# First set of the last product: its sums of h by chunks through PSUM, its weight sums behind the mask group's, the mask count later

## The chip, the core and the metric

The kernel runs on one core of a Trainium2 chip. The metric is device time in microseconds (us), the median of several runs. One further execution was recorded by the hardware profiler; its own time and its span, from the first to the last instruction, are given beside the median below. All instants in this document are microseconds from the start of that span.

The engines are called by their names: TensorE (PE in the profile; PEld is its weight load), VectorE (DVE), ScalarE (ACT), GpSimd (POOL) and SyncE (SP), which here only issues DMA transfers.

## The reference

Everything is fp32. There are 2 x 1024 tokens of 512 features, and the inner size of the gated layer is 1792.

```python
xn = layernorm(x)
block_mask = mask.reshape(16, 32, 16, 32).sum(axis=(1, 3)) > 0
s  = xn @ (weight * spread(block_mask)).T         # 512 -> 512
nx = xn * rsqrt(mean(xn ** 2) + 1e-5) * ln_w
h  = silu(nx @ gate_w.T) * (nx @ up_w.T)          # 512 -> 1792
g  = silu(h @ down_w.T)                           # 1792 -> 512
out = x + s * g
```

## The kernel before

**Products.** Every large product is split twice into 2 x 2 blocks, and at each of the two levels seven products of sums of blocks stand in for eight products of blocks (a Strassen scheme in Winograd's form). The outer level gives seven sets, numbered 1 to 7; inside a set, the inner level again gives seven products, also numbered 1 to 7. Numbers 1, 2 and 3 take blocks as they are on the side of the data; 5, 6, 7 and 4 take sums, and there 6 is formed from 5 and 4 from 6. On the weights' side 1, 2 and 4 take blocks and 5, 6, 3, 7 take sums.

**Stages.** Groups 0 to 6 are seven slices of gate and up weights, group 7 is the masked linear layer. First all groups run sets 1 and 2, then each group runs sets 6, 5, 7, 3, 4. One set of one group is an *instance*: seven products of 128x128 by 128x512 over seven positions. The last instances are those of group 7, the *mask group*. Then comes the *last product*, h by the down weights: seven sets in the order 1, 2, 6, 5, 7, 3, 4, of 25 products each (the very last ones are cut into narrower parts). For each set its h is loaded back from memory (`load_h`), its weights too (`load_d`), `inner_h` makes the four sums of h, and `inner_d` the four sums of the weights, on GpSimd.

**Order.** Each piece of work is put down with a position, `at(pos, fn, ...)`; at the end all pieces are sorted by position and issued in this order, so the order on every engine is written by hand. One position is about one product of TensorE. `END` is the position of the first product of set 1 of the last product; `D(o)(k)` is the position of product k of the o-th set. An engine works through its own pieces strictly in that order and waits where an input isn't there or a target is still read.

**Buffers.** One large tile `mem` of SBUF is cut into slots of 128x512, which are reused: `F["vc"]`, `F["a1"]` and so on are first slots of rings. PSUM banks are taken in turn from X (3 banks), Y (2), Z (1) and V (2). X, Y and Z hold running products; V holds whatever is short-lived: gates, copies of weights, the mask count `pm`. VectorE and ScalarE read and write PSUM here, GpSimd works on SBUF alone.

**Inside an instance.** Product 1 starts bank X, 5 starts Y, ScalarE copies X to Z (`seed`), 2 adds to Z, 6 to X. Then VectorE (ScalarE in sets 1 and 5) takes a *snapshot* of X and of Y, after which 7 and 4 add to X and 3 to Y, and VectorE reads each *total*. So the product 7 must wait for the snapshot of X, and product 3 for the snapshot of Y. In the mask group, set 5 ends in tiles v5, and GpSimd adds v5 and the running tiles acc into a third place (`summed`); set 7 then overwrites acc, which its VectorE totals may do only after that GpSimd sum has read it, and GpSimd adds again. These are the eight *mask sums* of GpSimd, all 128x512.

**What the change touches.** `mask_blocks` (L302): one small product that counts the mask by blocks of 32, and VectorE's compare. `inner_h` (L528): the sums of h, one instruction of 128x1536 each (three slots). `inner_d` (L514): the weight sums, four GpSimd instructions of 128x384. The placing of these for the o-th set stands in the loop over `DOWN`. Earlier users of the slots matter too: `h_sum` is GpSimd's sum of h in groups 0 to 6, stored to memory from L458, and the tiles vc of group 6 lie in `F["vc"]`.

Of the kernel before, what the change touches and what calls it, by code (L numbers as in the profile page):

```python
# [11 lines left out]
ALU = mybir.AluOpType  # L12
# [19 lines left out]
def tile_masked_linear_gated_ffn(  # L32
# [11 lines left out]
    nc = tc.nc  # L44
# [23 lines left out]
    def at(pos, fn, *args):  # L68
        events.append((pos, len(events), fn, args))
# [11 lines left out]
    F = first_slot  # L81
# [6 lines left out]
    def slots(i, n):  # L88
        return mem[:, i : i + n, :]
# [3 lines left out]
    def bank(tag, name):  # L93
        return ps.tile([P, W], F32, tag=tag, name=name, bufs=PSB[tag])

    def add(eng, o, a, b, op=ALU.add):
        eng.tensor_tensor(o, a, b, op)  # L97

    dve, pool, act = nc.vector, nc.gpsimd, nc.scalar
# [379 lines left out]
    K3 = G // 2  # L479
    assert G == 2 * K3 + 1  # L480
    dq, ds, dh, dt = {}, {}, {}, {}
# [32 lines left out]
    def inner_d(q, i):  # L514
        s = slots(i, 3).rearrange("p s w -> p (s w)").rearrange("p (m k w) -> p m k w", m=4, k=K3)
        a11, a21, a12, a22 = (dq[q][:, k : k + K3, r : r + P] for k in (0, K3) for r in (0, P))
        ds[q] = {5: s[:, 0], 6: s[:, 1], 3: s[:, 2], 7: s[:, 3], 1: a11, 2: a12, 4: a22}
        return [lambda: add(pool, s[:, 0], a21, a22), lambda: add(pool, s[:, 1], s[:, 0], a11, ALU.subtract),
                lambda: add(pool, s[:, 2], a12, s[:, 1], ALU.subtract), lambda: add(pool, s[:, 3], a11, a21, ALU.subtract)]
# [8 lines left out]
    def inner_h(q, m, i):  # L528
# [3 lines left out]
                7: lambda: (b22, b12), 4: lambda: (b21, dt[q, 6])}[m]()  # L532
        add(dve, t, a, b, ALU.subtract)

    fin, at_later = {}, []

    def load_final(R, Hh, i, slot_s, slot_x):
# [117 lines left out]
    END = 7 * N  # L655
# [109 lines left out]
    for i, (R, K) in enumerate(QUADS):  # L765
        at(62, load_mask, R, K)
        at(68 + 1.5 * i, mask_rows, R, K)
    at(76, mask_blocks)
    at(120, rms_store)
    for t in range(NTT):  # L770
        at(END + 13, rms_rows, t)
# [9 lines left out]
    def D(o):  # L781
        return lambda k: free[25 * o + k] if 25 * o + k < 25 * len(DOWN) else free[25 * o + k - 1] + 1

    H0, H1 = F["B1"], F["B6"]
    TS = [F["B7"] + K3 * k for k in range(5)]
    first_t = F["q"] - 1, F["a1"]
    b11, b12, b21, b22, e0, e1 = (0, 0, K3), (1, 0, K3), (0, K3, 2 * K3), (1, K3, 2 * K3), (0, G - 1, G), (1, G - 1, G)
    QD, later = (F["a1"] + 4, F["acc"], F["s"] + 5), {}
    for o, q in enumerate(DOWN):
        if o == 0:  # L790
            parts = [(p, 7 * where[4, 6] + 4 * k) for k, p in enumerate((b11, b12, b22, b21, e0, e1))]
        elif o == 1:
            parts = [(p, END - 22 + 7 * p[0]) for p in (b11, b21, e0, b12, b22, e1)]
        else:
            d = D(o - 2)
            parts = [(b11, d(4)), (b12, d(4) + 0.1), (b21, d(14)), (b22, d(21)), (e0, d(25) + 1), (e1, d(25) + 1.1)]
        for part, pos in parts:
            at(pos, load_h, q, (H0, H1)[o % 2], part)
        for k, m in enumerate((5, 6, 7, 4)):
            pos = END + (-26, -17, -8, -5)[k] if o == 0 else D(o - 1)((3, 8, 12, 18)[k])  # L800
            at(pos + 0.3, inner_h, q, m, first_t[k] if o == 0 and k < 2 else TS[(4 * o + k + 3) % 5])
        at((END - 29.8, END - 14, END + 7)[o] if o < 3 else D(o - 2)(4), load_d, q, QD[o % 3])

        def weight_sums(q=q, i=F["q"] + 2 - 3 * (o % 2), o=o):
            for k, fn in enumerate(inner_d(q, i)):
                later[o, k] = fn
        for k in range(4):
            pos = END + (-22, -18, -11, -9)[k] if o == 0 else D(o - 1)(10) + 2.5 * k
            if k == 0:
                at(pos, weight_sums)  # L810
            at(pos, lambda o=o, k=k: later[o, k]())
# [81 lines left out]
```

## Time and profile before

| what | value |
|---|---|
| median of 3 runs (lowest, highest) | 521.33 us (521.26, 521.42) |
| the profiled execution, its own time | 520.12 us |
| its span | 518.3 us |
| TensorE busy | 507.8 us, 98% of the span |
| VectorE busy | 384.5 us, 74% |
| GpSimd busy | 341.8 us, 66% |
| ScalarE busy | 177.8 us, 34% |
| memory moved | 121.59 MB, mean 235 GB/s |
| granted TensorE clock | full |

In a line of a timeline the first number is the start, the second the length; then come the engine, the line of the kernel, the operation, and written<-read by the program's names. "xN" says that N like instructions are merged. In brackets stand the idle time of the engine ahead of the instruction and what ended it. Almost all additions have the line L97, since one helper issues them; they are told apart by engine, tiles and sizes. A line of the chain of waits has start, length and what was at work; "issue" is time in which nothing that the profile shows was waited for. The stretch around the last instances of the mask group lies between 330 and 368 us, the mask count at 85 us, the last product from 362 us on.

### The profile page before, as it was taken

How to read it: one execution, taken by the hardware profiler on the slowest of the kernel's cores; microseconds unless marked ns; L12 is line 12 of the kernel's file. 1: busy time of each engine (PE TensorE's matmuls, PEld its weight loads, DVE VectorE, ACT ScalarE, POOL GpSimd, SP SyncE). 2: the span in 40 equal slices, each digit the busy share in tenths (PEclk: the TensorE clock that was granted, in tenths of full speed). 3: DMA queues.
4: the chain of work that ended last, by engine and by line, in shares of the span. 5: the costliest groups of instructions: out<-in, count | busy, mean ns of one | idle time of the engine just before them, and what ended most of it. 6: DMA issues, size and time to landing. Idle time of an engine off the chain costs nothing. (4 is left out here: it accounts for less than half of the span.)

```text
span 518.3 us, 4933 instructions
## 1 busy us (share of the span) xinstructions
PE 507.8 (98%) x1277; PEld 231.2 (45%) x1277; DVE 384.5 (74%) x583; ACT 177.8 (34%) x340; POOL 341.8 (66%) x280
## 2 busy tenths in 40 slices
PE   8899999999999999999999999998999999999997
PEld 8444544444444444444444444433444444444444
DVE  5897789876886969789696978979646654467826
ACT  3657644542536344353634433320101101001111
POOL 4422239852695978869597789989553564739960
PEclk9999999999999999999999999999999999999999
DMA  8435465459158485666988466498997599476472
GB/s 293 153 122 203 163 219 212 178 204 330 75 204 288 158 283 182 231 237 212 390 313 298 168 239 245 184 333 316 330 381 272 183 355 347 158 254 195 157 236 82
DMA packets 60460, 121.59 MB, mean 235 GB/s; under 512 B 5760, under 2 KB 13328, under 8 KB 58384
## 3 DMA queue, kind: packets, MB, share of 16 engines
q1 hardware_dynamic: 60144, 120.75, 65.9%
q10 hardware_dynamic: 288, 0.52, 0.3%
q8 instruction: 10, 0.16, 0.1%
q14 instruction: 18, 0.15, 0.1%
HBM read 75.11 MB, written 46.15 MB: 234 GB/s over the span
## 5 line engine op out<-in xcount | busy, mean ns | idle before, releaser
L97 POOL TENSOR_TENSOR mem<-mem 128x512 f32<-128x512 f32 (+4 forms) x243 | 306.4, 1285 | 139.1 <-ACT mem L264 45.6
L343 PE MATMUL x<-mem 128*128 128x512 f32 x448 | 214.5, 595 | 1.8 <-DVE mem L97 1.7
L343 PEld LDWEIGHTS x<-mem 128*128 128x128 f32 x448 | 83.3, 190 | 109.7 <-issue 85.2
L97 DVE TENSOR_TENSOR mem<-x,mem 128x512 f32<-128x512 f32 x136 | 91.7, 683 | 40.9 <-PE x L343 39.3
L343 PE MATMUL y<-mem 128*128 128x512 f32 x224 | 114.6, 593 | 1.6 <-DVE mem L97 1.5
L97 DVE TENSOR_TENSOR mem<-mem 128x512 f32<-128x512 f32 (+2 forms) x64 | 83.8, 1315 | 7.7 <-PE dx L570 4.2
L570 PE MATMUL dx<-mem 128*128 128x512 f32 x174 | 78.3, 592 | 0.0
L97 DVE TENSOR_TENSOR mem<-y,mem 128x512 f32<-128x512 f32 x96 | 65.7, 684 | 10.7 <-PE y L343 8.8
L343 PEld LDWEIGHTS y<-mem 128*128 128x128 f32 x224 | 42.0, 190 | 53.9 <-issue 46.5
L350 ACT COPY z<-x 128x512 f32<-128x512 f32 x55 | 31.5, 573 | 99.8 <-PE x L343 92.4
L343 PE MATMUL z<-mem 128*128 128x512 f32 x112 | 57.3, 593 | 0.5 <-ACT z L350 0.5
L570 PEld LDWEIGHTS dx<-mem 128*128 128x128 f32 x174 | 33.1, 190 | 41.6 <-issue 40.7
L570 PE MATMUL dy<-mem 128*128 128x512 f32 x98 | 44.5, 592 | 0.0
L404 ACT ACTIVATE gate<-mem 128x512 f32<-128x512 f32 x56 | 33.1, 601 | 28.1 <-DVE mem L97 23.7
L409 DVE TENSOR_TENSOR mem<-gate,mem 128x512 f32<-128x512 f32 x56 | 38.1, 681 | 4.5 <-POOL mem L97 3.7
L543 POOL TENSOR_TENSOR mem<-mem 128x512 f32<-128x512 f32 x16 | 24.9, 1565 | 17.3 <-DMA mem<-s_dram 17.0
L343 PEld LDWEIGHTS z<-mem 128*128 128x128 f32 x112 | 21.0, 190 | 26.7 <-issue 23.7
L553 ACT ACTIVATE silu<-mem 128x512 f32<-128x512 f32 x15 | 9.0, 602 | 64.6 <-DVE mem L97 48.3
L97 DVE TENSOR_TENSOR mem<-z,mem 128x512 f32<-128x512 f32 x41 | 28.0, 682 | 4.3 <-PE z L343 3.0
L570 PEld LDWEIGHTS dy<-mem 128*128 128x128 f32 x98 | 18.6, 190 | 23.4 <-issue 23.2
L97 DVE TENSOR_TENSOR mem<-dx,mem 128x512 f32<-128x512 f32 x16 | 11.0, 690 | 20.1 <-PE dx L570 20.1
L570 PE MATMUL dz<-mem 128*128 128x512 f32 x56 | 25.2, 592 | 0.0
(69 smaller groups left out, 280.2 us busy)
## 6 DMA issues: line engine op xcount, KB each, us to landing
h_dram<-mem SPq DMA_DIRECT2D x98, 256.0 KB, 2.1
mem<-h_dram SPq DMA_DIRECT2D x28, 768.0 KB, 6.4
mem<-in_gu SPq DMA_DIRECT2D x42, 256.0 KB, 4.1
acc_dram<-mem SPq DMA_DIRECT2D x8, 1024.0 KB, 4.0
mem<-acc_dram SPq DMA_DIRECT2D x8, 1024.0 KB, 4.9
s_dram<-mem SPq DMA_DIRECT2D x16, 256.0 KB, 2.4
mem<-s_dram SPq DMA_DIRECT2D x16, 256.0 KB, 6.6
mem<-in_x_t SPq DMA_DIRECT2D x16, 256.0 KB, 6.5
```

The costliest lines, as they stand in the source:

```text
L97: eng.tensor_tensor(o, a, b, op)
L343: nc.tensor.matmul(st[key], weights(g, q, m), operand(q, m), start=first and not (key == "z" and seeded), stop=True, skip_group_check=True)
L350: nc.scalar.copy(st["z"], st["x"])
L404: nc.scalar.activation(gate[key], t(), AF.Silu)
L409: nc.vector.tensor_mul(a(), gate[key], b())
L543: at_later.append(lambda: nc.gpsimd.tensor_tensor(s_tile, s_tile, rms_bc[t], ALU.mult))
L553: nc.scalar.activation(b[0][:, part], y[:, part] if source is None else source(), AF.Silu)
L570: nc.tensor.matmul(st[key], w(), b(), start=first and key != "z", stop=True, skip_group_check=True)
```

## The change

Three things change, all in order and slots; what is computed stays.

- **Sums of h of set 1.** The sums numbered 5 (b12 - b11) and 7 (b22 - b12) share the operand b12. Before, each was one 128x1536 instruction, at END - 25.7 and END - 7.7. Now they are made by three chunks of 128x512 each: ScalarE copies the chunk of b12 into a V bank, and VectorE makes both sums of that chunk from the bank, at END - 22.95, - 15.95 and - 8.95. Sum 6 goes from END - 16.7 to END - 1.95, sum 4 from END - 4.7 to END + 7.5. Sum 7 lies in the slots of the old vc, where it was in those of B7.
- **Weight sums of set 1.** The four GpSimd instructions go from END - 22, - 18, - 11, - 9 to END - 6, - 4.8, + 2, + 4, which is behind all eight mask sums. The load that feeds them keeps its place.
- **The mask count** goes from position 76 to 79.5, four products later.

On the engines this adds three ScalarE copies, and six VectorE sums of 128x512 for two of 128x1536. No transfer is added, removed or reordered.

```diff
+    def first_h(q, k, i5, i7):
+        st = {}
+        def in_bank():
+            st[0] = bank("V", f"h_{k}")
+            nc.scalar.copy(st[0], dh[q][:, 1, k, :])
+        def sums():
+            for m, i in ((5, i5), (7, i7)):
+                dt.setdefault((q, m), slots(i, K3))
+            add(dve, dt[q, 5][:, k, :], st[0], dh[q][:, 0, k, :], ALU.subtract)
+            add(dve, dt[q, 7][:, k, :], dh[q][:, 1, K3 + k, :], st[0], ALU.subtract)
+        return in_bank, sums
...
-    at(76, mask_blocks)
+    at(79.5, mask_blocks)
...
-    first_t = F["q"] - 1, F["a1"]
+    first_t = {5: F["q"] - 1, 7: F["vc"], 6: F["a1"], 4: TS[1]}
...
         for k, m in enumerate((5, 6, 7, 4)):
-            pos = END + (-26, -17, -8, -5)[k] if o == 0 else D(o - 1)((3, 8, 12, 18)[k])
-            at(pos + 0.3, inner_h, q, m, first_t[k] if o == 0 and k < 2 else TS[(4 * o + k + 3) % 5])
+            if o:
+                at(D(o - 1)((3, 8, 12, 18)[k]) + 0.3, inner_h, q, m, TS[(4 * o + k + 3) % 5])
+            elif m in (6, 4):
+                at(END + {6: -1.95, 4: 7.5}[m], inner_h, q, m, first_t[m])
+        if o == 0:
+            for k in range(K3):
+                in_bank, sums = first_h(q, k, first_t[5], first_t[7])
+                at(END - 24.4 + 7 * k, in_bank)
+                at(END - 22.95 + 7 * k, sums)
...
         for k in range(4):
-            pos = END + (-22, -18, -11, -9)[k] if o == 0 else D(o - 1)(10) + 2.5 * k
+            pos = END + (-6, -4.8, 2, 4)[k] if o == 0 else D(o - 1)(10) + 2.5 * k
```

## The prediction

> **What bounds the kernel now.** I read the page first, then TensorE's timeline for its gaps, then the chain of waits around each gap, then the timelines of the engines named there.
>
> From the page, the busy shares:
>
> ```profile
> PE 507.8 (98%) x1277; PEld 231.2 (45%) x1277; DVE 384.5 (74%) x583; ACT 177.8 (34%) x340; POOL 341.8 (66%) x280
> ```
>
> TensorE is the bound. Each product is two rows, which start 0.43 us apart when nothing holds them (0.86 us a product), so time can only come from the places where that beat breaks. TensorE's timeline (start, length, idle before it and what ended it), in three stretches:
>
> ```profile
> 83.21 1.13 PE L343 MATMUL x<-mem 128*128 128x512 f32 x2
> 85.10 0.41 PE L304 MATMUL pm<-mask_sums,blockones 128*128 128x64 f32 x2 [0.76 <-DVE mem L409]
> 85.34 0.65 PE L343 MATMUL y<-mem 128*128 128x512 f32 x1
> ...
> 347.35 1.02 PE L343 MATMUL x<-mem 128*128 128x512 f32 x2
> 349.39 0.70 PE L343 MATMUL x<-mem 128*128 128x512 f32 x1 [1.02 <-DVE mem L97]
> ...
> 358.93 1.02 PE L343 MATMUL x<-mem 128*128 128x512 f32 x2
> 361.42 0.70 PE L343 MATMUL y<-mem 128*128 128x512 f32 x1 [1.47 <-DVE mem L97]
> ```
>
> Counted by beat: the product at 347.35 should be followed at 348.21, the next comes at 349.39 (1.18 lost); at 358.93 it should be 359.79, it is 361.42 (1.63); the mask count pm should start at 84.18 (its forerunner's second row starts at 83.75), it starts at 85.10 (0.92). After a gap the first row takes 0.53 instead of 0.43 (0.10 more). From 362.4 to 511 no gap is shown.
>
> The chain of waits says where the two late gaps come from:
>
> ```profile
> 337.68 5.86 DMA mem<-in_down
> ...
> 344.62 1.28 POOL mem L97
> 345.90 0.02 issue
> 345.92 0.07 DVE mem L97
> 345.99 0.54 issue
> 346.53 2.81 DVE mem L97 x2
> 349.34 0.04 issue
> 349.39 1.13 PE x L343 x2
> ...
> 354.66 6.72 DVE mem L97 x5
> 361.38 0.04 issue
> 361.42 1.12 PE y L343 x2
> ```
>
> First gap: GpSimd stands at a weight sum of the last product until its load lands at 343.54; the mask group's sum behind it ends at 345.90 and frees the tile that VectorE then overwrites; VectorE's next instruction is a 128x1536 sum of h (2.20); only behind it comes the snapshot that the product at 349.39 needs. Second gap: two 128x1536 sums of h (2.41, 2.57) stand in front of the y snapshot.
>
> [...] (GpSimd, equal sums):
>
> ```profile
> 338.42 2.80 POOL L97 TENSOR_TENSOR mem<-mem 128x512 f32<-128x512 f32 x1
> 350.77 1.27 POOL L97 TENSOR_TENSOR mem<-mem 128x512 f32<-128x512 f32 x1
> ```
>
> The 2.80 lies over the first h sum (337.85 to 340.08). [...] here the sums with a PSUM input take 0.68 beside a busy GpSimd. [...] the trace has 0.68 and, undisturbed, 1.75 (364.98). [...]
>
> **The change part by part.**
>
> (1) Mask count four products later. One pm product, one VectorE compare, no DMA. pm now waits for a PSUM bank of the V pair, last read by the gate product at 84.27 to 84.95. In the new order y, x, x, y precede pm: it comes at 84.18 + 4 x 0.86 = 87.6, when bank and sums are ready. Gain 0.92. Its own 0.24 stays. VectorE's wait of 0.59 in front of the compare goes too, and what follows it stands about a microsecond earlier, as TensorE now asks. The compare ends at about 88.9; GpSimd's masking, its first reader, begins at 94.16.
>
> (2) Sums of h for sets 5 and 7 by chunks. Removed: two 128x1536 VectorE sums in the mask group (2.23 and 2.41). Added: three ScalarE copies of 0.58 (price of the like copies at L257) and six VectorE sums of 0.68, 0.60 apart, so 3.6 on VectorE in three bursts of 1.2. The copies are free: ScalarE works 6.3 of the 32.6 us from 329.8 to 362.4. Behind the first copy (about 338.6) stands the x copy of 339.82, which still waits for TensorE then. The first burst waits for more: its second sum writes the slots of the old vc, still read by group 6's last h sum on GpSimd and by a store. That store was issued at 337.27 and took 2.2 to land (339.4); the GpSimd sum would end at 338.42 + 1.27 = 339.7 now that no 1536 sum blocks it. So the burst ends near 340.6, and the next VectorE instruction was not due before 340.68. The later bursts fall at about 346.5 and 352.5, each behind the snapshot that TensorE needs next.
>
> (3) The other h sums. Set 6 moves to near the end: it follows the snapshot x of the last instance and runs about 358.5 to 360.3 (2.5 at most if blocked); its reader is the ninth product from the first of set 1. Set 4 moves into the last product, near 365.3 to 367.1 beside TensorE; its reader comes near 379. Behind it on VectorE stand two sums for the second set, needed beyond 380, and on SP the rms rows, whose slots it reads (issue at 370.30 before; TensorE's own reading ends near 369 now), so no queue moves back.
>
> (4) Weight sums behind the mask sums. Four GpSimd sums of 0.99 each leave the middle of eight 128x512 sums. The mask sums then follow their inputs: the first at 341.0 (its copy on ScalarE ends at 340.89), the one that freed VectorE at 345.90 by 342.3; the last waits for VectorE at about 354.3 and ends at 355.6 instead of 361.89. The weight sums then run 355.6 to about 359.6, or 361 if set 6's sum blocks one. The first is needed at 362.8, the second at 366.2. The load itself stays where it was on SP.
>
> TensorE's new beat: the product of 349.39 comes at 348.21 (its snapshot ends near 346.5), that of 361.42 at 358.50 (its snapshot ends at 356.8), the last product begins at 359.36 instead of 362.38. Gain: 1.18 + 0.10 + 1.63 + 0.10 = 3.01, plus 0.92, is 3.93. The small gaps of each group (0.3 with its slow row at 330.07) are left.
>
> Unknown costs. A sum with one input in PSUM and one in SBUF is in the trace (0.68), so is the copy; both ends are the same. That pm's gain of 0.92 passes through 240 us of other groups isn't shown: I take all of it, since the chain of every later gap goes back to TensorE's own products; the ends are 0 and 0.92. VectorE's burst beside TensorE: 0 to 0.5 lost; I take 0.
>
> Profiled execution: span 518.3, so 514.4, with the 1.8 around it (520.12) 516.2. The runs' median is 521.33, 1.21 above that execution; so 521.33 - 3.93 = 517.4.
>
> **The rivals.**
>
> A, a new small wait: a burst meets a snapshot that TensorE needs. Against it, the margins of 1.7 at both former gaps; for it, the small gaps in all groups, where VectorE is a few tenths late. Costs 0.3 to 1.2: 517.7 to 518.6.
>
> B, pm's gain is swallowed: a late engine between 85 and 330 makes TensorE wait later. Against it, results of that time are done well ahead: GpSimd's first masked weights at 95.22, for products that begin near 104. 518.3.
>
> C, slower: the store of the old vc lands late. On SP it stands right in front of the big load:
>
> ```profile
> 337.27 0.32 SPq L458 DMA_DIRECT2D h_dram<-mem  x1
> 337.68 0.38 SPq L489 DMA_DIRECT2D mem<-in_down  x1
> 338.50 0.32 SPq L458 DMA_DIRECT2D h_dram<-mem  x1
> ```
>
> The store of 338.50 took 6.1 to land, behind that load. If the first shared this fate (near 345), VectorE would stand 5 us with four instructions behind the burst's last sum, the x_2003, y_2048 and x_2038 totals among them; the product of 345.63 would wait for the last until about 347.8, 2.2 late, and the gain fall to 1.7 (519.6). Every further microsecond counts in full: from a landing at about 347.1 the change loses, and at 349 the time is 523. Against it: SP issues in order, and the store has 0.4 us of lead.
>
> D, the change does nothing: both gaps stay because VectorE is late from its total work. Against it, VectorE is idle for 5.0 of the 32.6 us there, and of the 9.4 us of its four 1536 sums 2.4 are over the undisturbed 1.75 each. 521.3.
>
> **How the numbers follow.** This forecast 0.63 (517.4, own range 517.0 to 517.7); A 0.12; B 0.08; a partial loss in C to 520 0.03; D 0.05; slower by C or an unseen wait 0.09. A range of 516.8 to 519.4 leaves the last three and a little out. A measurement of this kernel can tell about 0.2% (1 us) from no change. Faster than 520.3: 0.63 + 0.12 + 0.08 + 0.03 = 0.86, less 0.01 of A that comes out worse than its price: 0.85; same, D and that, 0.06; slower 0.09.
>
> **What would show it.** Right: no TensorE gap over 0.2 between 331 and 362; pm with no idle before it; the first dx product near 358.4 (both gains); GpSimd's eighth mask sum ending near 354.7, no 2.8 sums there. Wrong: a VectorE idle of microseconds in front of the second chunk sum (C), dy waiting for GpSimd's first weight sum, or gaps that return to TensorE before 330 (B).

## The result, and the profile after

The changed kernel takes 516.44 us (median of 4 runs, 516.12 to 516.81), the kernel before 521.3 (4 runs: the three known ones and one of 519.86). The ratio is 0.9913, 95% interval 0.9895 to 0.9932: 4.5 us faster, between 3.5 and 5.5. (The medians are 4.9 apart, the means of the same runs 4.5; the run of 519.86 moves the mean and hardly the median.) The forecast was faster, 517.4 within 516.8 to 519.4; the time lies 0.36 us below that range. The profiled execution took 516.81 with a span of 515.0; against the profiled execution of before, 518.3, that is 3.3.

The page after, TensorE's busy time and the others':

```profile
PE 507.4 (99%) x1277; PEld 231.5 (45%) x1277; DVE 383.6 (74%) x587; ACT 179.3 (35%) x343; POOL 339.3 (66%) x280
```

TensorE's timeline after, at the three places where it had gaps:

```profile
87.53 0.33 PE L304 MATMUL pm<-mask_sums,blockones 128*128 128x64 f32 x2
...
347.11 1.88 PE L343 MATMUL x<-mem 128*128 128x512 f32 x4
...
358.26 1.02 PE L343 MATMUL y<-mem 128*128 128x512 f32 x2
359.12 1.02 PE L586 MATMUL dx<-mem 128*128 128x512 f32 x2
```

No line has an idle time in brackets. The mask count comes at 87.53, without a wait in front of it. The four rows from 347.11 are two products; between them, where 1.18 us were lost, nothing is lost now. The two rows from 358.26 are the product in front of which 1.63 were lost. The last product begins at 359.12, 3.26 earlier than before.

VectorE after, at the first former gap:

```profile
344.80 0.69 DVE L97 TENSOR_TENSOR mem<-z,mem 128x512 f32<-128x512 f32 x1 [0.24 <-PE z L343]
345.59 0.69 DVE L97 TENSOR_TENSOR mem<-x,mem 128x512 f32<-128x512 f32 x1
346.20 0.68 DVE L97 TENSOR_TENSOR mem<-h,mem 128x512 f32<-128x512 f32 x1
```

The total of z waits for TensorE and no longer for GpSimd; the snapshot of x ends at 346.28, and the chunk of h stands behind it. So the forecast steps are there. But 0.92 + 3.01 is more than the 3.3 of the two spans. The rest was lost at a place that the forecast named only in its case B. TensorE's timeline near 257 us, after, and one line of it before:

```profile
257.48 1.13 PE L343 MATMUL z<-mem 128*128 128x512 f32 x2 [0.24 <-ACT z L350]
258.44 1.02 PE L343 MATMUL x<-mem 128*128 128x512 f32 x2
259.89 1.13 PE L343 MATMUL x<-mem 128*128 128x512 f32 x2 [0.43 <-DVE mem L97]
```

```profile
259.00 2.24 PE L343 MATMUL x<-mem 128*128 128x512 f32 x4
```

By the beat the two waits after cost 0.40 + 0.60 = 1.0. Before, one wait of 0.26 stood there: the four rows at 259.00 take 0.36 longer than the 1.88 of four rows without a wait, and 0.10 of that is the slow first row. The change edits nothing at this place, and the experiments had to say what the wait is.

### The profile page after: what moved, and what is told of

The parts are those of the page before. It is cut to its first block, busy times and chain, and to the rows that moved or that the text cites. A ratio compares the mean times of both kernels' runs of the same rounds, so it can differ in the third digit from the quotient of the medians.

```text
span 515.0 us, 4942 instructions
## 1 busy us (share of the span) xinstructions
PE 507.4 (99%) x1277; PEld 231.5 (45%) x1277; DVE 383.6 (74%) x587; ACT 179.3 (35%) x343; POOL 339.3 (66%) x280
## 5 line engine op out<-in xcount | busy, mean ns | idle before, releaser
L97 DVE TENSOR_TENSOR mem<-mem 128x512 f32<-128x512 f32 (+3 forms) x62 | 78.7, 1277 | 6.9 <-PE dx L586 3.6
L559 POOL TENSOR_TENSOR mem<-mem 128x512 f32<-128x512 f32 x16 | 24.7, 1545 | 16.7 <-DMA mem<-s_dram 16.6
```

Source lines behind the costliest of these rows:

```text
L559: at_later.append(lambda: nc.gpsimd.tensor_tensor(s_tile, s_tile, rms_bc[t], ALU.mult))
```

## The experiments

The kernel before was measured beside them on the same chip: 520.67 (36 runs) for the first four, 520.53 (22) for the next four, 520.66 (9) for the last four. In the ratios below it is the divisor. "Wait at 257" is TensorE's loss between 250 and 262 us without the slow first rows, and gaps are counted by the beat of 0.43 us, both in the one profiled execution of each kernel.

**1. The kernel before, repeated.** No edit.

> The kernel before once more, unchanged, to find the 1.2 us by which its median (521.3) exceeds its profiled execution (520.12). Theory 1, the excess lies in the two late gaps that the change removes: an execution near 521.3 shows the gaps at 349 and 361 longer by 1.2 us together. Theory 2, it lies in another place, where a transfer lands at a time of its own (the weight blocks near 257): there the gaps add up to 1.2 us more than the 0.26 of the first profile. Theory 3, it belongs to the occasion and not to the kernel: then all executions of this call stand near 519.9 to 520.2, and the changed kernel gains 3.4 to 3.9 us beside them.

Measured: 520.94 (21 runs, 519.94 to 522.2), ratio 1.0005 (0.9998 to 1.0012). Its profiled execution was by chance the longest of them, 522.2, span 520.3. The count's gap is 0.92, the two late ones are 1.28 and 1.64, so only 0.11 of the 2.0 us by which this span exceeds the first lies there. The wait at 257 is 1.86 against 0.26, in two pieces of about 1.3 and 0.6, and so makes 1.6 of the 2.0. TensorE and ScalarE of this execution:

```profile
259.62 1.13 PE L343 MATMUL z<-mem 128*128 128x512 f32 x2 [1.11 <-ACT z L350]
...
262.03 1.12 PE L343 MATMUL x<-mem 128*128 128x512 f32 x2 [0.42 <-DVE mem L97]
```

```profile
254.18 1.70 ACT L264 ACTIVATE mem<-mem,lnw_sb 128x256 f32<-128x256 f32 x4 [2.73 <-DMA mem<-in_gu]
...
258.98 0.59 ACT L350 COPY z<-x 128x512 f32<-128x512 f32 x1
```

ScalarE waits 2.73 us for the weight blocks of a gate and up group (L264 scales them), and the copy that TensorE's z needs is queued behind the scaling. That is the place of theory 2: the times of the kernel before would spread with the landing of this load. Experiments 6 and 7 test that.

**2. The count four products later, alone.**

```diff
-    at(76, mask_blocks)
+    at(79.5, mask_blocks)
```

> The mask count four products later, alone. If the 0.92 us passes through to the end: 0.9 faster than before. If it is swallowed where TensorE waits for the weight blocks near 257 us: the gap at 85 is gone, new gaps of some 0.8 us stand between 250 and 262, and the time is 0.0 to 0.3 us better.

Measured: 519.68 (16 runs), ratio 0.9980 (0.9973 to 0.9988), so 1.0 faster (0.6 to 1.4). The gap at 85 is gone; the wait at 257 is 1.10, within what executions of the kernel before show (0.26 to 1.86). The median says that the 0.92 passes through; one profile alone would have said that most of it is swallowed.

**3. The sums of h alone.** The changed kernel with two edits taken back:

```diff
-    at(79.5, mask_blocks)
+    at(76, mask_blocks)
...
-            pos = END + (-6, -4.8, 2, 4)[k] if o == 0 else D(o - 1)(10) + 2.5 * k
+            pos = END + (-22, -18, -11, -9)[k] if o == 0 else D(o - 1)(10) + 2.5 * k
```

> The sums of h by chunks, sums 6 and 4 later; the weight sums stay between the mask sums and the count where it was. If VectorE's long sums of h are what turns GpSimd's lateness into a TensorE gap: GpSimd still waits for the load until about 343.5, VectorE's total for it until 345.9, but the snapshot follows at once and ends at 347.2, ahead of 348.21, so both late gaps go and it is 3.0 us faster. If the weight sums are needed for the first gap: it keeps 1.18 + 0.10, and is 1.7 us faster.

Measured: 517.42 (5 runs), ratio 0.9940 (0.9927 to 0.9954): 3.1 faster (2.4 to 3.8). Both late gaps are gone from the profile, the count's gap of 0.92 is there. So the weight sums need not be moved to close the first gap.

**4. The changed kernel, repeated.** No edit.

> The changed kernel once more, beside the kernel before on one chip. If the sum of the prediction holds within one occasion: 3.9 us faster, less what TensorE waits between 250 and 262 (0.8 in the first profile of it, 0.26 in that of before), so 3.4 to 3.9. If the change also removes the 1.2 us of the median: 4.6 to 5.1.

Measured: 516.06 (4 runs, 515.91 to 516.56), ratio 0.9913 (0.9900 to 0.9927): 4.5 faster (3.8 to 5.2). Its profile has no late gap, and a wait at 257 of 0.40. The interval overlaps both expected ranges, the lower one only just, and so does not decide between them.

**5. The weight sums alone**, on the kernel before.

```diff
-            pos = END + (-22, -18, -11, -9)[k] if o == 0 else D(o - 1)(10) + 2.5 * k
+            pos = END + (-6, -4.8, 2, 4)[k] if o == 0 else D(o - 1)(10) + 2.5 * k
```

> The weight sums behind the mask sums, alone; the sums of h whole and where they were, the count where it was. If GpSimd's place in the queue is the root of both late gaps: VectorE's total at 345.9 comes at 345.0 and its long sum ends near 347.9, so the snapshot ends at 348.5 and the first gap falls from 1.18 to about 0.3; without GpSimd's work beside them the two later sums take 1.75 to 2.2 each, and the second gap falls from 1.63 to 0 to 0.6: about 2.2 us faster. If the long sums of h make the second gap by themselves: only the first shrinks, about 1 us faster.

Measured: 518.49 (6 runs), ratio 0.9962 (0.9949 to 0.9975), 2.0 faster (1.3 to 2.7). The first gap is gone, the second is 0.97. VectorE and TensorE:

```profile
345.26 1.75 DVE L97 TENSOR_TENSOR mem<-mem 128x1536 f32<-128x1536 f32 x1
346.93 0.69 DVE L97 TENSOR_TENSOR mem<-x,mem 128x512 f32<-128x512 f32 x1
...
355.85 2.58 DVE L97 TENSOR_TENSOR mem<-mem 128x1536 f32<-128x1536 f32 x1
358.36 0.68 DVE L97 TENSOR_TENSOR mem<-y,mem 128x512 f32<-128x512 f32 x1
```

```profile
359.09 0.70 PE L343 MATMUL y<-mem 128*128 128x512 f32 x1 [0.81 <-DVE mem L97]
```

Either edit removes the first gap by itself: there the long sum in front of the snapshot is harmless if GpSimd is in time (the snapshot ends at 347.62, its product starts at 347.82), and GpSimd's lateness is harmless if no long sum follows it. The second gap shrinks because one of the two sums now takes 1.75, but the other still takes 2.58 in front of the snapshot.

**6 and 7. The loads of h for set 1 nine positions later**, on the changed kernel and on the kernel before. In both:

```diff
-            parts = [(p, 7 * where[4, 6] + 4 * k) for k, p in enumerate((b11, b12, b22, b21, e0, e1))]
+            parts = [(p, 7 * where[4, 6] + 9 + 4 * k) for k, p in enumerate((b11, b12, b22, b21, e0, e1))]
```

> The changed kernel with the six loads of h for set 1 nine positions later, so that none of them stands in front of group 5's weight blocks on SP. If the varying wait near 257 us comes from the second of these loads (landing at 250.7 to 252.9 in the profiles so far, the blocks right behind it): no gap over 0.2 between 250 and 262, 0.3 to 0.7 us faster than the changed kernel, near 515.5, with less spread. If ScalarE's own work makes that wait: as the changed kernel, 516.1.

> The kernel before with the same later loads of h. If the loads are the cause of the wait near 257: about 0.7 us faster than the kernel before (its runs lie that far above what its profile without this wait gives), and the distance to the changed kernel with later loads is the 3.9 us of the sum with nothing added. If the distance is 4.5 or more, a part of the change's gain isn't in the sum.

Measured on the changed kernel: 515.32 (4 runs, 515.03 to 515.78), ratio 0.9898 (0.9884 to 0.9912). On the kernel before: 519.57 (16 runs), ratio 0.9981 (0.9973 to 0.9988). In both profiles TensorE keeps its beat from 250 to 262 us. ScalarE of the changed kernel with later loads:

```profile
250.14 1.71 ACT L264 ACTIVATE mem<-mem,lnw_sb 128x256 f32<-128x256 f32 x4
...
255.76 0.59 ACT L350 COPY z<-x 128x512 f32<-128x512 f32 x1
```

The scaling begins straight after the copy ahead of it, four microseconds earlier than in the repeated kernel before (about one of the four because TensorE itself is that much earlier here). The four block loads take 3.9 us to land (median); behind the load of h they took 6.3 in the first profile of before, 7.9 in its repetition, 7.3 in the first profile after. So the wait is that of loads issued behind a 768 KB load (at 244.50, 6.5 us to land, in the first profile of before; the blocks from 246.16 on); the edit moves all six loads of h, and that this one matters is read from the traces. Moving them gains 1.0 (0.6 to 1.4) on the kernel before and about 0.7 on the changed one. Of this 0.2 lies elsewhere: TensorE's small wait near 269 us falls from about 0.31 to 0.14 in both kernels. The runs of the kernel before also draw together, from 2.1 us between lowest and highest (22 runs) to 0.9 (16). The distance of the two kernels is now 4.25, between the two values that were expected, and with an uncertainty of over half a microsecond it excludes neither; the gaps of this kernel-before profile (0.92, 1.41, 1.62 and 0.10 twice for the slow row) add up to 4.15.

**8. The big load in front of the store** (case C), on the changed kernel.

```diff
-        at((END - 29.8, END - 14, END + 7)[o] if o < 3 else D(o - 2)(4), load_d, q, QD[o % 3])
+        at((END - 31, END - 14, END + 7)[o] if o < 3 else D(o - 2)(4), load_d, q, QD[o % 3])
```

> The changed kernel with the big load of set 1's weights one place earlier on SP, in front of the store of the old vc (case C of the prediction made true). If the first chunk's second sum waits for that store: it waits on VectorE until about 344.3, the product of 345.4 until 346.9, a gap of 1.5 there, 1.5 us slower than the changed kernel. If the slot isn't what holds that sum: as the changed kernel.

Measured: 516.57 (5 runs), ratio 0.9922 (0.9910 to 0.9935), 0.5 above the changed kernel with overlapping intervals. VectorE:

```profile
342.49 0.69 DVE L97 TENSOR_TENSOR mem<-mem,h 128x512 f32<-128x512 f32 x1 [3.40 <-DMA h_dram<-mem]
```

The wait is the one foreseen, the cost isn't: TensorE lost 0.21, not 1.5. The big load left at 335.49, two microseconds sooner than expected, so the store behind it (issued at 336.43, 6.0 us to land) landed at 342.4 and not 344.3. The chain from there was right: four VectorE instructions, this sum the first of them, end at 344.97, and the product that was due at 344.81 came at 345.03.

**9. The chunks without the copies**, on the changed kernel.

```diff
-            st[0] = bank("V", f"h_{k}")
-            nc.scalar.copy(st[0], dh[q][:, 1, k, :])
+            st[0] = dh[q][:, 1, k, :]
```

> The changed kernel with the chunks kept and the copies to PSUM left out: the six chunk sums take both operands from SBUF. If the copies matter [...]: sums of up to 1.9 on VectorE or 2 on GpSimd where they meet, a TensorE gap of 0.3 to 1 us near 348, and as much slower than the changed kernel. If the placing alone matters: longer single sums in the first two bursts, but no gap over 0.2, and 516.1 within 0.2 us.

Measured: 516.28 (5 runs), ratio 0.9917 (0.9904 to 0.9931), as the changed kernel. VectorE in the second burst, two sums:

```profile
345.71 2.86 DVE L97 TENSOR_TENSOR mem<-mem 128x512 f32<-128x512 f32 x2
```

They take 2.86 instead of the 1.28 of the same two with the copies (346.20 to 347.48 in the first profile after). There GpSimd sums lie over this stretch, at 345.57 and 347.11; whether such sums lengthen the two here is not shown. No gap follows, since the snapshot stands ahead of them.

**10. The weight sums back in their old places**, on the changed kernel: the second edit of experiment 3 alone.

> The changed kernel with the weight sums back between the mask sums. If VectorE's long sums alone turned GpSimd's lateness into TensorE's gaps: GpSimd waits for the load until about 343.3 again, VectorE's total comes near 345.6 instead of 344.6, no gap, and 516.1 as the changed kernel. If the moved weight sums carry the first gap: 1.2 us slower than the changed kernel.

Measured: 516.92 (5 runs), ratio 0.9931 (0.9919 to 0.9944), overlapping that of the changed kernel. VectorE's total of z waits for GpSimd until 345.74 again, the snapshot ends at 347.03 for a product that starts at 348.04, and no late gap is in the profile; its wait at 257 is 0.81, twice that of the repeated changed kernel. By the profile the moved weight sums add nothing. By the times up to 0.9 stays open: all five runs (516.56 to 517.31) lie above all five of experiment 9 on the same chip (516.04 to 516.46). In the two profiles this difference stands at 257, where none of the moved instructions is; why it does is not shown.

**11. Sums 6 and 4 of h moved, and nothing else**, on the kernel before.

```diff
-            pos = END + (-26, -17, -8, -5)[k] if o == 0 else D(o - 1)((3, 8, 12, 18)[k])
+            pos = END + (-26, -2.25, -8, 7.2)[k] if o == 0 else D(o - 1)((3, 8, 12, 18)[k])
```

> The kernel before with one edit: sums 6 and 4 of h, whole as they were, at END - 1.95 and END + 7.5; sums 5 and 7 whole at their old places, weight sums and count as before. If the two long sums just ahead of the snapshots make both gaps: sum 6 no longer stands in front of the snapshot (it ends at 347.2, due 348.2), and with sum 7 alone the y snapshot ends near 357.3, due 358.5; no gap over 0.2, 3.0 us faster than the kernel before. If one long sum in front of the y snapshot is enough for a gap: 0.3 to 1 us less than that.

Measured: 517.30 (5 runs), ratio 0.9939 (0.9927 to 0.9952), 3.2 faster (2.5 to 3.8). VectorE where the second gap was:

```profile
353.49 2.12 DVE L97 TENSOR_TENSOR mem<-mem 128x1536 f32<-128x1536 f32 x1
...
356.74 0.68 DVE L97 TENSOR_TENSOR mem<-y,mem 128x512 f32<-128x512 f32 x1
```

Sum 7 is whole and takes 2.12, against 1.75 for a sum of this size while GpSimd is idle (364.98 in the first profile of before), and still the y snapshot ends at 357.4 for a product at 358.62. TensorE keeps its beat from 331 to the end. The chunks, the copies and the new place of sum 7 are not what gains the 3 us; taking the other two long sums away from the snapshots is.

**12. Three placings.** The edit of 11, the count later (2), the loads of h later (6).

> The edit of the last kernel, with the count four products later and set 1's loads of h nine positions later: no chunks, no copies, no weight sums moved. If these three placings are all that counts: the same 515.3 as the changed kernel with later loads, 0.7 below the changed kernel. If chunks and copies carry a part of the gain: above 515.7.

Measured: 515.49 (4 runs, 515.43 to 515.53), ratio 0.9903 (0.9890 to 0.9917), against 0.9898 (0.9884 to 0.9912) for experiment 6. The same, with no added instruction, 5.1 us below the kernel before. It is below the changed kernel too, but by the later loads of h, which that kernel does not have.

## Why the prediction was right or wrong

**What bounds it, and where the time is lost:** right. All three gaps went with the edits that were named for them, and the new beat holds: bursts of h sums at 338.98, 346.20 and 352.21, the weight sums of GpSimd from 355.39 to 361.02. The forecast instants of the snapshots of x and y (346.5 and 356.8) leave out the 0.92 of the count; the signs that include it were a first dx product near 358.4 and GpSimd's eighth mask sum ending near 354.7. In the first profile after these came at 359.12 and 355.43, late by what was lost near 257; in the repeated one (experiment 4), where less was lost there, at 358.49 and 354.79.

**(1) The count, 0.92:** right in size (experiment 2: 1.0, 0.6 to 1.4). That it passes through was a choice between 0 and 0.92; the medians bear it out, though the wait at 257 hides it in single executions.

**(2) to (4), 3.01 for the late gaps:** right in mechanism, slightly short in size. The first gap was read from one execution as 1.18; three others of kernels with this gap show 1.23, 1.28 and 1.41, with GpSimd's wait for the load 2.7 us long in the one of 1.41 (experiment 7) against 2.46. The forecast took all parts together and did not ask which of them a gap needs. Experiments 3, 5, 10 and 11 show that for the first gap either part would do, and that moving sums 6 and 4 alone closes both. The copies and chunks, worked out at length, were not needed. That a VectorE sum with an input in PSUM leaves GpSimd its pace was the author's estimate, from such sums at 0.68 beside GpSimd (356.99 before); in the first profile after, the GpSimd sum that took 2.80 at 338.42 before takes 1.27 at 338.18, with the first chunk sum (338.98, 0.69) over its end.

**The step that failed** is "The runs' median is 521.33, 1.21 above that execution; so 521.33 - 3.93 = 517.4". It took 521.33 for the level of the kernel before, and the 1.21 for a fixed offset that both kernels carry. The level was about 0.7 too high: three runs had 521.33; 36, 22 and 9 later ones have 520.5 to 520.7. And what lies above the execution that I read is no fixed offset: executions differ mainly by the wait at 257 us, which was 0.26 in that one and is 1.86 in one that took 522.2, and with that wait gone (experiment 7) the median is 519.57. From 520.5 to 520.7 the same sum gives 516.6 to 516.7, just below the range's low end and 0.2 to 0.7 above the two medians of the changed kernel. Of what remains the longer first gap is 0.05 to 0.23; that the wait at 257 costs the changed kernel 0.3 less than the one before is measured from few runs and stays open. Open too is why all three given runs lay so high: of 88 executions of the same kernel in and beside the experiments 13 reach 521.26.

**Rivals.** A didn't come. B seemed to come in the first profile after (0.74 more at 257 than in that of before), but the medians speak against it (experiment 2 gained 1.0, at least 0.6): its place was that of the varying load. C was made true in experiment 8; its chain holds, its landing did not: at a wait of 3.40 on VectorE TensorE lost only 0.21, and a later landing was not tried. D is refuted by every experiment with a late gap gone. In the range I had priced new waits and not the one already there, whose spread the three given runs (521.26 to 521.42) didn't show, but the 1.2 between them and the profiled execution did.

## What to carry to other kernels

When a profiled execution is shorter than the median of a few runs, do not carry the difference over as an offset: ask which wait in the trace depends on the landing of a transfer, give the range its spread, and take the level from more than three runs. When a bound engine waits for a short read-out, look at what long piece stands in front of that read-out in its engine's order; moving that piece can be worth all that a finer split would gain (3.2 and 3.1 us here, experiments 11 and 3). Take a load that nobody needs for long out of the way of one that is about to be needed: here that was worth 0.7 to 1 us and most of the spread.

## What the runs showed of the hardware that I had not expected

- The landing of the same four 256 KB loads, issued from 246.16 and from 246.6 on and behind the same 768 KB load, had medians of 6.3 and 7.9 us in two executions of one kernel; with the large load out of the way 3.9.
- Two 128x512 sums on VectorE with both inputs in SBUF took 2.86 us (experiment 9, 345.71), the same two with one input in PSUM 1.28 (the first profile after, 346.20). Two others of the first kind in experiment 9 took 1.14 (337.13) and 0.69 (339.43).
